# A four-layer graph attention kernel: the next unit's row spread earlier in PE's order, and the tail's masks half by DMA, half by ScalarE

## The chip, the cores and the metric

The kernel runs on one core of a Trainium2 chip. Its engines work side by side, each through its own instructions in order: TensorE (PE) multiplies matrices, VectorE (DVE), ScalarE (ACT) and GpSimd (POOL) do elementwise work, and SyncE (SP) issues nearly all DMA transfers. They wait for each other through semaphores. The metric is the time of one execution on the device in microseconds, as the median of several runs.

## The reference, in short

The input is `x`, 8 graphs of 2048 nodes with 64 features, and one adjacency matrix `adj` of 2048 by 2048. Four layers follow each other, each wrapped as `x = layernorm(x + layer(x, adj))`. Layers 0 to 2 are graph attention:

```python
h = matmul(x, W)                       # layer 0 also scales x and normalises h
s1, s2 = h @ a1, h @ a2
e = leaky_relu(s1[:, :, None] + s2[:, None, :], 0.2)
att = softmax(where(adj > 0, e, NEG_BIG), axis=-1)
out = elu(matmul(att, h))              # layer 0 adds h before the elu; layer 2 has relu
```

Layer 3 is an attention with a score of its own for every feature:

```python
feat = softplus(x * (w0 / sqrt(2)) + b0)
scores = feat * wa + ba
attn = softmax(where(mask, scores, -1e9), axis=2)
out = einsum('bijd,bjd->bid', attn, feat)
```

Because these scores don't depend on the receiving node, layer 3 is two masked sums: of exp(score) and of exp(score) times feature, over the neighbours, and their ratio.

## The kernel before, in words

**Units and tiles.** The list `todo` holds 24 units, a unit being one layer (0, 1 or 2) of one graph `b`: layers 0 and 1 of graphs 0 to 3, layers 0 and 1 of graphs 4 to 7, and then layer 2 of all eight. A unit has K = 16 tiles, one for each block of 128 sending nodes. For tile `jb`, `weights` has DVE make a weight tile `w` of 128 senders by 2048 receivers (the larger of a row and a limit, times the 0/1 edge tile); in layer 2 `exponential` then has ACT apply exp. `products` has PE multiply it with the features into the sums `acc`. There are four buffers for `w`. The text names a tile by its unit and `jb`: tile 15 is the last of a unit, "1_4" is layer 1 of graph 4.

**The row and its spread.** What DVE compares against is a row of 2048 numbers that is the same on all partitions. It lies in PSUM as `r`, in one single buffer, and `spread` writes it with four matmuls of a 3-row bf16 operand (`row3`) against ones. So the spread of the next unit must wait until DVE has read `r` for tile 15, and the first tile of the next unit (tile 0) must wait for the spread. `spread_for` does it once per unit, provided that the unit is `prepared` (its row is on its way in by DMA).

**The order of the work.** The kernel's text is run once, and every engine's instructions are kept in the order in which it emits them. The main loop goes through units `n` and tiles `jb`, and a pass is called a step here. A step calls `reach` (which emits the weights up to this tile, in layer 2 up to two tiles ahead, and the exponentials up to one ahead), then `products`, then `bg.step()`. `bg` is the side work: generators for finishing a unit (`finish`: copying `acc` to `oT`, transposing to `p_o`, dividing by `den`, normalising), for `scores` of the next layer (`p_xT`, `p_s`, `s`, `se`, `s_top`, `p_r`), for features, for the group statistics of layer 2 (`p_lse`), and for layer 3. Each goes on by one piece per step. SP's order is not fixed this way: its transfers stand in the order in which a planner expects them to become possible.

**Where the spread stood.** `reach` called `spread_for(n + 1)` as soon as it had emitted the weights of tile 15. In layers 0 and 1 that is at the start of step 15, behind the side work of step 14. In layer 2, where weights run two tiles ahead, it is in step 13, ahead of the products of tile 13.

**Layer 3 and the tail.** Graphs go in pairs. `l3_features` makes features for a graph (`sp`, `x`, `d`, `fs`, `fm`, and the high and low halves `v`), and `l3_products` goes through 64 blocks, 16 of receiving nodes for each of four pairs. A block is 32 matmuls with the mask of its nodes as the stationary operand, and ACT copies the result to `nd`. Every two blocks `l3_finish` makes the output: it loads two pieces of `e` by DMA, takes the reciprocal, multiplies (`o`), adds `e`, squares on ACT (`sq`), normalises and stores. Beside layer 2, masks come by DMA as f32 from `mask_d`, which the kernel wrote to DRAM earlier, four pieces of 256 KB for a block, in five buffers (`fetch`, asked for by `widen`). The tail is what is left when layer 2 has ended: the blocks from 33 on, with the finish of the last unit and the features of graphs 6 and 7 among them. There `widen` made a mask out of the fp8 edge matrix: ACT for the even blocks, POOL for the odd ones, in two buffers.

All engine calls pass through a helper, so that the profile has line L80 for nearly everything; the names of the tiles tell them apart.

Of the kernel before, what the change touches and what calls it, by code (L numbers as in the profile page):

```python
# [50 lines left out]
def gnn4_kernel(ctx: ExitStack, tc: tile.TileContext, t, out):  # L51
# [3 lines left out]
    K = N // P  # L55
# [51 lines left out]
    class Banks:  # L107
# [4 lines left out]
        pool = None  # L112
# [28 lines left out]
    pe, dve, act, pool = (InOrder(e) for e in (nc.tensor, nc.vector, nc.scalar, nc.gpsimd))  # L141
# [74 lines left out]
    src = t["L0_gnn_a"]  # L216
# [63 lines left out]
    def mask(p, jb):  # L280

        for h in range(2):
            dve.tensor_scalar(
                edge[:, jb, h * (N // 2) : (h + 1) * (N // 2)],
                raws[jb][h], 0.0, None, ALU.is_gt, saturate=False,
            )
        if jb < 6:
            load_raw(jb + 6)
        elif jb >= 10:
            load_raw(jb + 2)  # L290
        if jb == K2:
            load_x(2)
        if jb >= K - 3:
            load_x(jb - K + 6)
        if jb == 0:
            pe.matmul(p[:, : 2 * K], lhsT=edge[:, 0, :P], rhs=zeros_h, start=True, stop=False)
        for ib in range(K):
            pe.matmul(
                p[:, 2 * ib : 2 * ib + 2],
                lhsT=edge[:, jb, ib * P : (ib + 1) * P],  # L300
                rhs=ones_h,
                start=False,
                stop=False,
            )
        if jb == K - 1:
            pe.matmul(p[:, : 2 * K], lhsT=edge[:, 0, :P], rhs=zeros_h, start=False, stop=True)
# [504 lines left out]
    def ready(layer, b):  # L811
        return (layer, b) in V and hasattr(S.get((layer, b)), "row")
# [17 lines left out]
    def spread(layer, b):  # L830

        sc = S[layer, b]
        sc.r = Banks.r
        for c in range(NCH):
            sl = slice(c * 512, (c + 1) * 512)
            pe.matmul(sc.r[:, sl], lhsT=ones3, rhs=sc.r3[:, sl], start=True, stop=True)
# [134 lines left out]
    def unit(layer, b):  # L971
        u = Unit()
        u.layer, u.b, u.n = layer, b, f"{layer}_{b}"
        u.s, u.w = S[layer, b], {}
        return u

    def sums_of(u):
        u.acc = [psA.tile([P, 512], F32, tag="acc", name=f"acc_{u.n}_{c}") for c in range(2)]
# [5 lines left out]
    def weights(u, jb):  # L984

        s = u.s
        w = u.w[jb] = work.tile([P, N], F32, tag="w", name=f"w_{u.n}_{jb}", bufs=4)
        low = s.low if u.layer == 2 else s.e[:, 1]
        for sl in halves(u, jb):
            dve.scalar_tensor_tensor(  # L990
                w[:, sl], s.r[:, sl], low[:, jb : jb + 1], edge[:, jb, sl], ALU.max, ALU.mult
            )

    def exponential(u, jb):

        w = u.w[jb]
        for sl in halves(u, jb):
            act.activation(w[:, sl], w[:, sl], AF.Exp, bias=u.s.down[:, jb : jb + 1])

    units, prepared, spreads = [], set(), {0}  # L1000

    def spread_for(n):
        if n in spreads:
            return
        spreads.add(n)
        if n == 1:
            Banks.use("psR", 1)
            Banks.r = Banks.pool.tile([P, N], F32, tag="b", name="r")
        spread(*todo[n])
# [3 lines left out]
    def reach(t):  # L1013

        while front[0] < K * len(todo):
            n, jb = divmod(front[0], K)
            layer, b = todo[n]
            if n not in prepared or front[0] > t + (2 if layer == 2 else 0):
                break
            if jb == 0:  # L1020
                spread_for(n)
                units.append(unit(layer, b))
            weights(units[n], jb)
            front[0] += 1
            if jb == K - 1 and n + 1 in prepared:
                spread_for(n + 1)
        while behind[0] < min(front[0], t + 2):
            n, jb = divmod(behind[0], K)
            if todo[n][0] == 2:
                exponential(units[n], jb)  # L1030
            behind[0] += 1

    def products(u, jb):

        s, w = u.s, u.w[jb]
        sums = [u.acc[c // 2][F * (c % 2) : F * (c % 2) + F, :] for c in range(NCH)]
        for c in range(NCH):
            pe.matmul(
                sums[c],
                lhsT=s.v[:, jb, :],  # L1040
                rhs=w[:, c * 512 : (c + 1) * 512],
                start=(jb == 0),
                stop=False,
            )
        if jb == K - 1:

            assert s.whole
            for c in range(NCH):
                rows = slice(32 * c, 32 * c + 3)
                pe.matmul(sums[c], lhsT=s.mean[rows], rhs=emptyT[rows], start=False, stop=True)  # L1050
# [124 lines left out]
    now = [0, 0, 0]  # L1175
# [82 lines left out]
    def widen(block):  # L1258

        if block >= K * B // 2:  # L1260
            return
        ib = block % K
        src = edge[:, :, ib * P : (ib + 1) * P]
        if now[0] == 3:
            m = work.tile([P, K, P], F32R, tag="row", name=f"mask_{block}")
            if block % 2:
                pool.tensor_copy(m, src)
            else:
                act.copy(m, src)
            wide[block] = [m[:, r * K8 : (r + 1) * K8] for r in range(4)]  # L1270
            return
        wide[block] = [None] * 4
        asked.extend((block, r) for r in range(4))
# [125 lines left out]
    def chain(*gens):  # L1399
        for g in gens:  # L1400
            if isinstance(g, int):
                yield g
            else:
                yield from g()
# [26 lines left out]
    def flags():  # L1431

        for layer in range(2):
            dve.tensor_scalar(s_top[:, layer], s_top[:, layer], -S_MAX[layer], None, ALU.add)
        top = small.tile([P, 2], F32, tag="top", name="top")
        dve.tensor_reduce(top[:, 0:1], s_top, AX.XY, ALU.max)
        yield 1
        yield from pm_slots.take()
        p = psum("p_top")
        pe.transpose(p[:1, :P], top[:, 0:1], ident)  # L1440
        yield 1
        dve.tensor_reduce(top[0:1, 1:2], p[:1, :P], AX.X, ALU.max)
        pm_slots.give()
        dve.tensor_tensor(beyond[0:1, :], beyond[0:1, :], top[0:1, 1:2], ALU.max)
        dve.tensor_scalar(flag, beyond[0:1, :], 0.0, None, ALU.is_gt)
# [3 lines left out]
    for n, (layer, b) in enumerate(todo):  # L1449
        if (layer, b) == (2, 1):  # L1450
            early_.close()
            late = ctx.enter_context(tc.tile_pool(name="late", bufs=1))
            bg.add(l3_products())
        if (layer, b) == (2, 5):
            bg.add(flags())
        now[:] = layer, n, 0
        nxt = todo[n + 1] if n + 1 < len(todo) else None
        done = nxt is None

        for jb in range(K):  # L1460
            if n == 0:
                while masks < min(K, 9 + jb):
                    mask(p_deg, masks)
                    masks += 1
                if jb == K - 3:
                    empties(p_deg)
            now[2] = jb
            reach(K * n + jb)
            u = units[n]
            if jb == 0:  # L1470
                sums_of(u)
            products(u, jb)
            if jb == K - 1:
                end = [lambda u=u: finish(u)]
                if layer < 2:
                    end += [2 if now[0] < 2 else 1, lambda layer=layer, b=b: scores(layer + 1, b)]
                else:
                    end += [1, lambda b=b: l3_features(b)]
                if layer == 1 and b % NB == NB - 1:
                    end += [lambda b=b: group(b // NB)]  # L1480
                bg.add(chain(*end), begun=True)
            elif not done and jb >= 10 and ready(*nxt):
                prepare(*nxt)
                prepared.add(n + 1)
                done = True
            if layer == 0 and jb == 2 and 6 <= b + 4 < B:
                load_x(b + 4)
            if n == 0 and jb == 3:
                bg.add(constants())
            if n == 9 and jb == 3:  # L1490
                bg.add(mask_out())
            if (n, jb) in begin:
                bg.add(features0(begin[n, jb]))
            bg.step()
        while not done:
            bg.step()
            if ready(*nxt):
                prepare(*nxt)
                prepared.add(n + 1)
                done = True  # L1500
# [509 lines left out]
```

## Time and profile before

| | us |
|---|---|
| median of 3 runs | 1392.18 (1391.94 to 1396.22) |
| the profiled execution | 1391.82 |
| its span, first to last instruction | 1390.0 |
| PE busy | 1220.5 (88%) |
| DVE busy | 1214.1 (87%) |
| POOL busy | 817.7 (59%) |
| ACT busy | 751.3 (54%) |
| spread, 92 matmuls | 25.3 |
| masks cast by POOL, 16 | 30.5 |
| masks cast by ACT, 15 | 28.4 |

Times in the profile count from the first instruction. A group's row gives how many instructions there were, their busy time and mean, and the idle time of the engine just before them with what ended it. A row of the waits reads: engine and tile that waited, what it waited for, total us, number of times, longest. The chain that ended last runs from the last instruction back to whatever released each step. A matmul of f32 operands shows as several records. PE's busy time counts modelled ends, so that a busy PE isn't at its peak everywhere.

### The profile page before, as it was taken

To read this page: it belongs to the slowest core of one execution; us is meant where nothing else is said; L and a number is where in the kernel's file an instruction comes from. 1 tells how busy PE (TensorE), PEld (TensorE's weight loads), DVE (VectorE), ACT (ScalarE), POOL (GpSimd) and SP (SyncE) were. 2 spreads that over 40 slices of the span, in tenths; PEclk is the share of its full clock that TensorE was granted. 3 is DMA by queue.
4 is the path that set the end of the run, shared out by engine and by line. 5 is a ranking of instruction groups with operands and counts; after the bars stand their busy time and mean duration, and the time that the engine had idled before them with its cause. 6 is when DMAs were issued, how large, how long until landed. Compare 5 with 4: busy or idle time off the path is not lost.

```text
span 1390.0 us, 19341 instructions
## 1 busy us (share of the span) xinstructions
PE 1220.5 (88%) x7169; PEld 623.5 (45%) x7169; DVE 1214.1 (87%) x1108; ACT 751.3 (54%) x1369; POOL 817.7 (59%) x1103
## 2 busy tenths in 40 slices
PE   3689898999898979999997879799989899976996
PEld 3333233333343423343332324255644455666996
DVE  3889889999999999889999899998879798877876
ACT  4444543446245544343436987867666768564432
POOL 1566777558668686756743543343646564676665
PEclk9799999999999999999999989899999899998998
DMA  8640000000000212123101000034443444511111
GB/s 298 227 93 1 1 2 1 1 2 2 1 1 1 91 62 77 62 77 93 32 2 39 1 16 2 21 107 133 138 122 97 123 123 136 162 25 32 35 39 34
DMA packets 112010, 87.24 MB, mean 63 GB/s; under 512 B 57917, under 2 KB 90845, under 8 KB 110882
## 3 DMA queue, kind: packets, MB, share of 16 engines
q1 hardware_dynamic: 111538, 85.79, 20.6%
q8 instruction: 59, 0.97, 0.3%
q14 instruction: 45, 0.37, 0.1%
q10 hardware_dynamic: 368, 0.12, 0.0%
HBM read 60.40 MB, written 25.45 MB: 62 GB/s over the span
## 4 chain that ended last, share of the span: by engine, by line
PE 29%; DVE 15%; ACT 5%; issue 4%; POOL 2%; POOLq 0%; DVEq 0%; ACTq 0%
PE p_l L80 14%; PE acc L80 12%; DVE w L80 8%; DVE o L80 2%; ACT w L80 1%; PE p_o L80 1%; DVE nd L80 1%; DVE x L80 1%; ACT sp L80 1%; DVE fs L80 1%; PE r L80 1%; POOL sq_x L80 1%; POOL st_x L80 0%; PE p_s L80 0%; ACT L80 0%
## 5 line engine op out<-in xcount | busy, mean ns | idle before, releaser
L80 DVE SCALAR_TENSOR_TENSOR w<-r,se,edge 128x2048 f32<-128x2048 f32 (+1 forms) x270 | 552.7, 2101 | 32.2 <-PE r L80 24.5
L80 PE MATMUL acc<-w,pv 128*64 128x512 f32 x2048 | 498.9, 621 | 52.8 <-DVE w L80 41.1
L80 DVE SCALAR_TENSOR_TENSOR w<-r,lo_g,edge 128x2048 f32<-128x2048 f32 (+1 forms) x144 | 297.6, 2097 | 22.1 <-PE acc L80 12.0
L80 ACT ACTIVATE w<-w,down_g 128x2048 f32<-128x2048 f32 (+1 forms) x144 | 257.2, 1810 | 69.2 <-DVE w L80 59.7
L80 PEld LDWEIGHTS p_l<-v,mask 128*128 128x128 f32 x2048 | 256.4, 196 | 61.9 <-issue 47.8
L80 PE MATMUL p_l<-v,mask 128*128 128x256 f32 x2048 | 271.2, 291 | 10.6 <-POOL mask L80 7.0
L80 PEld LDWEIGHTS acc<-w,pv 128*64 128x64 f32 x2048 | 133.0, 139 | 312.4 <-issue 181.0
L80 PE MATMUL acc<-w,x 128*64 128x512 f32 x1024 | 259.1, 637 | 14.5 <-ACT w L80 10.8
L80 POOL TENSOR_TENSOR sq_x<-sq_x 128x32 f32<-128x32 f32 (+4 forms) x207 | 110.0, 532 | 64.8 <-ACT sq_x L80 50.3
L80 PEld LDWEIGHTS acc<-w,x 128*64 128x64 f32 x1024 | 67.0, 142 | 132.0 <-issue 89.2
L80 ACT ACTIVATE o<-p_o,den 128x64 f32<-128x64 f32 x256 | 55.9, 327 | 72.5 <-DVE den L80 72.5
L80 ACT ACTIVATE nd<-p_l,empty 128x256 f32<-128x256 f32 x64 | 30.1, 470 | 109.3 <-PE p_l L80 109.3
L80 PE MATMUL p_o<-rh,oT 128*128 128x130 f32 x384 | 60.1, 293 | 21.1 <-DVE o L80 5.8
L80 PEld LDWEIGHTS p_o<-rh,oT 128*128 128x128 f32 x384 | 49.3, 194 | 54.9 <-issue 34.3
L80 ACT COPY oT<-acc 128x512 f32<-128x512 f32 x48 | 25.6, 585 | 87.9 <-PE acc L80 87.9
L80 POOL TENSOR_TENSOR eh<-eh,x 128x1024 f32<-128x1024 f32 (+2 forms) x24 | 36.4, 1531 | 61.2 <-ACT eh L80 56.7
L80 POOL TENSOR_TENSOR st_x<-isw_x,mhalf 128x16 f32<-128x16 f32 x24 | 70.6, 2940 | 1.9
L80 POOL TENSOR_TENSOR d<-x,wa_bc 128x1024 f32<-128x1024 f32 x8 | 19.0, 2376 | 68.5 <-DVE x L80 68.5
L80 DVE RECIPROCAL nd<-nd 128x256 f32<-128x256 f32 x32 | 55.7, 1742 | 0.0
L80 POOL TENSOR_TENSOR sq_x<-o 128x512 f32<-128x512 f32 x23 | 29.3, 1272 | 41.5 <-DVE o L80 41.3
L80 ACT ACTIVATE xs<-x,nodes 128x64 f32<-128x64 f32 x128 | 44.2, 434 | 3.6 <-PE p_xT L80 3.6
L80 POOL CAST mask<-edge 128x2048 fp32r<-128x2048 fp8e4 x16 | 30.5, 1906 | 24.1 <-PE p_l L80 24.1
(260 smaller groups left out, 1558.4 us busy)
## 6 DMA issues: line engine op xcount, KB each, us to landing
mask<-mask_d SPq DMA_DIRECT2D x132, 256.0 KB
mask_d<-mf SPq DMA_DIRECT2D x32, 512.0 KB
raw<-in_adjT_dram SPq DMA_DIRECT2D x8, 1024.0 KB
raw<-in_adjT_dram SPq DMA_DIRECT2D x16, 512.0 KB
x<-in_x_dram SPq DMA_DIRECT2D x8, 512.0 KB
x_d<-x SPq DMA_DIRECT2D x8, 512.0 KB
e<-x_d SPq DMA_DIRECT2D x64, 64.0 KB
out_dram<-o SPq DMA_DIRECT2D x64, 64.0 KB
```

What stands on the lines that cost most here:

```text
L80: ins = f(*args, **kwargs)
```

## The change

Three edits. `reach` no longer emits the spread behind the weights of tile 15. The main loop does, right behind the products of one tile and ahead of that step's side work: in layers 0 and 1 behind tile 14, for which it first has `reach` emit the weights of tile 15 (at the end of layer 1 that also takes in the first two tiles of the coming unit, with their exponentials, since layer 2 runs ahead); in layer 2 behind tile 13. In the tail POOL makes no masks: the odd blocks' masks are made by ACT, and the even blocks' are asked for and fetched by DMA as beside layer 2.

```diff
@@ reach @@
             weights(units[n], jb)
             front[0] += 1
-            if jb == K - 1 and n + 1 in prepared:
-                spread_for(n + 1)
@@ widen @@
-        if now[0] == 3:
+        if now[0] == 3 and block % 2:
             m = work.tile([P, K, P], F32R, tag="row", name=f"mask_{block}")
-            if block % 2:
-                pool.tensor_copy(m, src)
-            else:
-                act.copy(m, src)
+            act.copy(m, src)
             wide[block] = [m[:, r * K8 : (r + 1) * K8] for r in range(4)]
             return
@@ the main loop @@
             products(u, jb)
+            if n + 1 in prepared and jb == K - (3 if layer == 2 else 2):
+                reach(K * n + jb + (0 if layer == 2 else 1))
+                spread_for(n + 1)
             if jb == K - 1:
                 end = [lambda u=u: finish(u)]
```

## The prediction

> **What bounds the kernel now.** I read the windows by stage first, then the chain that ended last, the groups, the waits, and for each place touched the timeline. The windows (start:end, length, then busy us of PE, PEld, DVE, ACT, POOL; clock; DMA share; GB/s) for layers 0 and 1, the last part of layer 2, the start of the tail and its steady part:
>
> ```profile
> 60.00:738.00 678.00, 623.36 (x3312) 242.37 (x3309) 629.26 (x462) 300.67 (x888) 456.20 (x622) 0.97 0.12 35
> 1017.00:1217.00 200.00, 187.22 (x1074) 109.16 (x1069) 168.14 (x167) 135.92 (x118) 112.07 (x157) 0.96 0.43 124
> 1217.00:1290.00 73.00, 52.20 (x364) 47.96 (x362) 58.05 (x77) 41.21 (x53) 50.36 (x45) 0.88 0.11 28
> 1290.00:1377.00 87.00, 86.22 (x704) 86.02 (x704) 66.82 (x118) 32.49 (x46) 54.44 (x66) 0.98 0.17 37
> ```
>
> In layers 0 and 1 VectorE (DVE) and TensorE (PE) are both near full. One tile is 2.26 us start to start on DVE, 1.87 us on PE; PE's spare time goes to side work. The tail's steady part is pure PE: 704 matmuls in 86.2 us, 3.92 us a block of 32. Before it PE idles over 20 us. The waits say what for:
>
> ```profile
> DVE w L80 <- PE r L80: 34.6, 17, 3.9
> PE r L80 <- DVE w L80: 12.9, 5, 5.0
> PE p_l L80 <- POOL mask L80: 7.0, 2, 6.2
> PE p_l L80 <- ACT mask L80: 2.4, 1, 2.4
> ```
>
> The first is DVE held at a unit's start by the spread, the second PE held in front of the spread. The group of casts that the change removes (count; busy us, mean ns of one; idle before):
>
> ```profile
> L80 POOL CAST mask<-edge 128x2048 fp32r<-128x2048 fp8e4 x16 | 30.5, 1906 | 24.1 <-PE p_l L80 24.1
> ```
>
> The tail's waits in place, with the neighbours that matter (start, duration, engine, instructions; in brackets the idle time before and its releaser):
>
> ```profile
> 1259.02 14.18 PE L80 MATMUL p_l<-v,mask 128*128 128x256 f32 x96 [6.19 <-POOL mask L80]
> 1277.20 0.43 PE L80 MATMUL p_fm<-fs,ones 128*128 128x64 f32 x2 [4.01 <-DVE fs L80]
> ...
> 1257.15 1.84 DVE L80 SCALAR_TENSOR_TENSOR st_x<-st_x 128x16 f32<-128x16 f32 x1 [2.37 <-POOL st_x L80]
> 1265.66 2.10 DVE L80 TENSOR_TENSOR o<-o,e 128x256 f32<-128x256 f32 x1
> ...
> 1257.08 1.89 POOL L80 CAST mask<-edge 128x2048 fp32r<-128x2048 fp8e4 x1
> 1265.59 1.89 POOL L80 CAST mask<-edge 128x2048 fp32r<-128x2048 fp8e4 x1 [0.31 <-PE p_l L80]
> ```
>
> A 128x16 operation took 1.84 us and ended as POOL's mask cast ended; elsewhere the same shape takes 0.15. The 128x256 one took 2.10, elsewhere 0.42. POOL's casts hold DVE, and the chain that ended last runs through just these DVE operations from 1229 to 1286.
>
> **What the Trainium skill says.** "SBUF — State Buffer", section "Who interferes with whom": a DVE instruction with two SBUF inputs and a GpSimd instruction that reads SBUF exclude each other, and whichever starts first holds the shared pair to its end. The trace agrees (1.84 against 0.15 us). The same section has DMA on ports of its own: from 920 to 1010 us mask fetches ran at 144 GB/s while PE was busy 90.00 of 90.00 us. "TensorE: Matmul & The Clock Gate", section "What's actually happening": an idle array falls to a slower clock and needs a busy stretch to recover. The block behind the 4.01 us wait took 5.56 us, not 3.92.
>
> **Spread in layers 0 and 1.** Four matmuls, 1.03 us, move ahead of the side work of step 14, with the weights of tile 15 on DVE; nothing is added, and no DMA moves with them. Of 16 unit changes, PE's order differs at eight: five are unchanged, three move only a 0.28 us mean on DVE. DVE's gap between tile 15 and the next tile 0 is 1.1 to 4.3 us, with a floor of 1.11 (at 739.60, where PE was ready). Above the floor lie 15.6 us. But side work displaced on PE is done all the same, so a gain counts only where DVE doesn't wait for PE soon after. By unit change, in order of time:
> - 0_1 to 0_2: PE was at p_mean; 0.36 us, given back at 183.43 where PE waits for POOL's tree. 0.
> - 0_2 to 0_3 and 1_5 to 1_6: 1.26 us each, but DVE's s_top soon waits for ACT's s, which is queued behind the oT copies that wait for PE's tile 15 (663.78: 1.90 us already). PE's total to there is the same. 0.
> - 1_1 to 1_2: p_xT of 1.38 us steps aside; DVE restarts at 318.2 instead of 319.53. 1.3.
> - 1_2 to 1_3: 1.03, but the next unit has no PE idle, so it returns as a wider gap at 401.86. 0.
> - 0_5 to 0_6: spread at 483.6 (tile 15's end) instead of 484.37. 0.7.
> - 0_7 to 1_4: PE now waits 0.37 for tile 15, and DVE waits for PE at 581.93 (1.81 us). A loss of 0.4.
> - 1_4 to 1_5: 32 lse matmuls (0.96) step aside; 0.9.
> - the three DVE moves: 0.3 together. In the one into layer 2, two tiles and their exponentials are also issued earlier on DVE and ACT; the mean's cast behind them waits 0.4 us at 744, covered by the 0.26 us waits that follow and oT.
> Sum: 1.3 + 0.7 - 0.4 + 0.9 + 0.3 = 2.8 us. Bounds: all of 15.6 if PE's catching up costs nothing, minus 3 if each of eight waits for tile 15 by 0.37.
>
> **Spread in layer 2.** It moves the other way, behind tile 13 (1.87 us), ahead of the side work of step 13. Where PE waited for tile 15, tile 13 fills the wait; where PE is full, the spread comes 1.87 us later and DVE's next tile with it.
> - 2_0 to 2_1: exponential 13 ends only at 779.18, so tile 13 ends at 781.07 and the spread is 0.66 later than 780.41. DVE is the chain there: a loss of 0.7.
> - 2_1 to 2_2: wait 4.30, but DVE does side work until 833.56. 0.
> - 2_2 to 2_3: wait 4.97; tile 14 must await its exponential (888.1); tile 15 and oT come 1.0 earlier, of which DVE takes its 0.57 wait for ACT's d. 0.6.
> - 2_3, 2_4 and 2_6: PE full. DVE's next tile comes 1.87 later, covered: its exponential is read at 952.6, 1015.1 and 1159.4, 4 to 7 us after it, and DVE itself then waits 2.2, 6.5 and 2.6 us for ACT's x. If that cover were gone, 1.87 each. 0.
> - 2_5 to 2_6: on the chain that ended last. Wait 1.01, then spread 1.02 and a slow tile 13 of 3.18. Tile 13's exponential was done at 1076.4, so it fills the wait; p_l starts at 1080.6 instead of 1082.9. 2.3.
> Sum: 0.6 + 2.3 - 0.7 = 2.2 us.
>
> **The tail's masks.** POOL loses 16 casts (30.5 us). ACT has 16 instead of 15, of 1.89 us, now the odd ones. SP gains 60 fetches of 256 KB, for the even ones. Where SP's fetches go: five buffers, so a fetch waits for a tile released two blocks, 7.8 us, before it is needed. Layer 2 needs a block per 7.9 us from the same five buffers, and PE's whole wait for them was 0.8 us. The rate is 1 MB per 7.84 us, 134 GB/s, plus 37 now, against 158 GB/s late in layer 2 and 298 at the start: I take its cost as nothing; the high end is in the rivals. On SP each fetch costs 0.32 us of issue, and loads and stores of the finish stand between them; the last fetches go out during blocks 60 and 61 of 63, so the last finish is untouched.
>
> What leaves: the 6.19 us wait would only become a longer wait for DVE's fs at 1277.20, since the matmul waiting there keeps its place. So the gain is what DVE gains. Casts held operations of the chain: x at 1229.06 by 0.5; st_x at 1257.15 by 1.7; o at 1265.66 by 1.7. (1.1 at 1241.60 goes to a wait for p_o.) So p_fm starts at 1277.2 - 3.9 = 1273.3. Then block 40 at the slow 5.6, block 41 without its 0.82 wait, block 42 fetched, no longer behind ACT's four casts: it starts at 1283.0 instead of 1290.28. Block 43 is new on ACT, queued behind sq, which waits for o of the finish. That is at 1293.3 now, minus 3.9, minus casts of 1.4 at 1282.21 and 1.7 at 1290.10: 1286.3; plus sq 0.4, nd 0.4, cast 1.9: 1289.0, 2.1 us after PE is ready (1286.9). Before, block 43 started at about 1294.5. Gain 5.5 us; without that new wait 7.3, with 5 us lost to lateness of fetches 0.5. From there PE sets the end in both.
>
> **Sum.** 2.8 + 2.2 + 5.5 = 10.5 us from the profiled execution's 1391.82 (span 1390.0 and 1.82 around it): 1381.3. The median of the runs shown is 0.36 above that execution: 1381.7.
>
> **Rivals.**
> - Partial (1388.5): the spread's gains all come back as waits for ACT's s, p_o or oT one step later, as they do at half of the unit changes already, and the tail gives 3.7. For it: PE idles only 2 to 5 us a unit. Against: DVE's gaps in the waits are real idle time of the busiest engine.
> - Slower (1399): fetches come late in the tail. One mechanism: SP takes its queue in order, and each block pair has a fetch behind a load of e that waits for DVE's o, or behind a store. Its margin is 7.8 us less the landing. If it is late by x, PE stalls x at each of 15 even blocks: 0.7 us eats the gain of 10.5, 1.0 us makes it slower than can be told from no change, 1.2 gives 1399. Against it: the finish has slack (DVE 66.8 of 87 us busy), and the worst such fetch that I find, the fourth of block 44 behind the loads of e at 1286.3, goes out near 1287.5 and is needed near 1296.
> - Larger (1373): PE's catching up costs little, half of the 15.6 us come, and mask 43 isn't late: 8 + 2.2 + 7.3 and about a microsecond of DVE holds.
> - The change not doing what it says: excluded for the order; for time it is the partial case.
>
> **How the numbers follow.** Forecast (1376 to 1386) 0.55, larger 0.12, partial (1386 to 1393) 0.24, slower 0.09. A difference under 0.3%, 4.2 us, can't be told from no change here. Faster (under 1388.0): 0.55 + 0.12 + 0.08 of the partial case = 0.75; slower (over 1396.4) 0.09; the rest 0.16. The range leaves out half of the larger case, the slower one and a fifth of the partial one: 1373.5 to 1391.
>
> **What would show it.** Waits of DVE w for PE r fall in layers 0 and 1 (24.5 to about 17 us), while those for ACT's s and p_o grow; in layer 2 they grow (10.1 to about 17), where they are covered. PE's waits in front of r fall from 12.9 to about 6. DVE's operations near 1257 and 1266 take 0.15 and 0.42 us. PE has no wait for POOL's mask, one of about 2 us for ACT's mask 43, and 9 us in front of p_fm. Over 1 us of waiting for the mask's DMA means the slower rival. The prediction is wrong if the tail's chain isn't DVE's, or if the time to 1217 doesn't fall.

## The result, and the profile after

The changed kernel takes 1380.24 us in the median of ten runs (1377.55 to 1384.78), the kernel before 1390.82 (1384.2 to 1396.22, ten runs beside them): a ratio of 0.9929, 95% interval 0.9913 to 0.9945, so 10.6 us less where the forecast had 10.5. The profiled execution took 1384.76 us, nearly the longest of the ten, and its span of 1383.0 is only 7.0 below the 1390.0 of before. So the two profiles can't be subtracted as wholes; they are read by stages.

The windows of the changed kernel, at the times and with the columns of the windows of before:

```profile
60.00:738.00 678.00, 621.47 (x3330) 243.96 (x3330) 632.16 (x462) 301.96 (x891) 457.90 (x626) 0.98 0.12 35
1017.00:1217.00 200.00, 187.15 (x1096) 109.77 (x1093) 170.63 (x170) 140.97 (x129) 117.37 (x161) 0.98 0.43 126
1217.00:1290.00 73.00, 54.56 (x392) 53.38 (x391) 56.82 (x90) 38.92 (x46) 40.49 (x41) 0.84 0.39 112
1290.00:1377.00 87.00, 78.77 (x653) 78.57 (x652) 57.43 (x117) 31.72 (x43) 34.77 (x57) 0.97 0.51 144
```

The last row has PE busy for 78.77 of 87 us, where it had 86.22. That isn't a slower tail, but one whose last matmul ends 78.77 us into the window, in place of 86.5. The DMA share there has gone from 0.17 to 0.51, POOL's work from 54 to 35 us.

The waits (engine and tile that waited, for what: total us, times, longest):

```profile
DVE w L80 <- PE r L80: 34.0, 17, 5.7
DVE den L80 <- PE p_o L80: 14.1, 10, 6.0
PE p_fm L80 <- DMA e<-x_d: 9.8, 1, 9.8
DVE s_top L80 <- ACT s L80: 3.3, 3, 2.2
PE p_l L80 <- ACT mask L80: 2.6, 1, 2.6
PE r L80 <- DVE w L80: 2.1, 5, 0.7
PE p_l L80 <- DMA mask<-mask_d: 0.4, 1, 0.4
```

DVE's wait for `r` is as long as before (34.0 against 34.6), but it has moved, as the two groups of weights (layers 0 and 1, then layer 2) show in their last column:

```profile
L80 DVE SCALAR_TENSOR_TENSOR w<-r,se,edge 128x2048 f32<-128x2048 f32 (+1 forms) x270 | 552.4, 2102 | 24.0 <-PE r L80 17.1
L80 DVE SCALAR_TENSOR_TENSOR w<-r,lo_g,edge 128x2048 f32<-128x2048 f32 (+1 forms) x144 | 297.3, 2096 | 25.5 <-PE r L80 16.9
```

It is 17.1 us in layers 0 and 1, from 24.5, and 16.9 in layer 2, where it is covered. PE has no wait for a mask of POOL's; it waits 9.8 us in front of the last `p_fm` and 2.6 for mask 43. (The waits put the first down to the load of `e`; PE's weight load of the same matmul, PEld, waits 10.0 for DVE's `fs`, which is what it needs.) These places in the timeline (start, duration, engine, instructions; in brackets the idle time before):

```profile
1232.42 5.76 PE L80 MATMUL p_l<-v,mask 128*128 128x256 f32 x32
1238.02 0.61 PE L80 MATMUL p_o<-rh,oT 128*128 128x130 f32 x4
...
1270.15 0.69 PE L80 MATMUL p_fm<-fs,ones 128*128 128x64 f32 x2 [9.81 <-DMA e<-x_d]
1270.15 0.50 PEld L80 LDWEIGHTS p_fm<-fs,ones 128*128 128x128 f32 x2 [10.01 <-DVE fs L80]
...
1253.43 0.17 DVE L80 SCALAR_TENSOR_TENSOR st_x<-st_x 128x16 f32<-128x16 f32 x1 [2.37 <-POOL st_x L80]
...
1260.29 0.42 DVE L80 TENSOR_TENSOR o<-o,e 128x256 f32<-128x256 f32 x1
```

The two operations that POOL's casts held take 0.17 and 0.42 us, where they took 1.84 and 2.10. But the block in front of the last unit's last `p_o` (the fourth of its four; the expectations below call it the third) took 5.76 us, not about 4, so `p_o` came later here. The next section shows why this matters.

For comparing profiles I use five marks that each of them has: the matmul that closes a unit (`acc` from `emptyT` and `mean`, here "last sum"), the last matmul of all (`p_l`), and the end of the span. The stages are A, from the second unit's last sum to that of layer 1 (unit 15, counted from 0); B, from there to that of unit 23; C, from there to the last `p_l`; D, the rest. Before: 597.5, 479.5, 155.6, 13.5. After: 595.4, 474.2, 153.9, 14.2. What lies ahead of A was 1.5 us longer in this profile. That is scatter: the first unit's last sum stands between 104.2 and 107.2 us in the profiles, whichever kernel it is, and the second unit takes 39.7 us in all of them.

### The profile page after: what moved, and what is told of

The parts are those of the page before. It is cut to its first block, busy times and chain, and to the rows that moved or that the text cites. A ratio compares the mean times of both kernels' runs of the same rounds, so it can differ in the third digit from the quotient of the medians.

```text
span 1383.0 us, 19457 instructions
## 1 busy us (share of the span) xinstructions
PE 1213.5 (88%) x7169; PEld 623.5 (45%) x7169; DVE 1200.7 (87%) x1108; ACT 753.3 (54%) x1370; POOL 790.3 (57%) x1087
## 4 chain that ended last, share of the span: by engine, by line
PE 43%; DVE 22%; ACT 7%; issue 6%; POOL 1%; DMA 0%; DVEq 0%; POOLq 0%; SPq 0%; ACTq 0%
PE acc L80 22%; PE p_l L80 14%; DVE w L80 14%; ACT w L80 2%; DVE o L80 2%; PE p_o L80 2%; PE p_s L80 1%; PE r L80 1%; ACT sp L80 1%; DVE nd L80 1%; DVE x L80 1%; PE p_lse_g L80 1%; DVE fs L80 1%; ACT L80 1%; DVE mean L80 1%
## 5 line engine op out<-in xcount | busy, mean ns | idle before, releaser
L80 DVE SCALAR_TENSOR_TENSOR w<-r,se,edge 128x2048 f32<-128x2048 f32 (+1 forms) x270 | 552.4, 2102 | 24.0 <-PE r L80 17.1
L80 PE MATMUL acc<-w,pv 128*64 128x512 f32 x2048 | 493.8, 615 | 53.8 <-DVE w L80 42.8
L80 DVE SCALAR_TENSOR_TENSOR w<-r,lo_g,edge 128x2048 f32<-128x2048 f32 (+1 forms) x144 | 297.3, 2096 | 25.5 <-PE r L80 16.9
L80 PE MATMUL acc<-w,x 128*64 128x512 f32 x1024 | 255.6, 627 | 25.3 <-ACT w L80 21.9
L80 POOL TENSOR_SCALAR isw<-isw 128x4 f32<-128x4 f32 x32 | 9.7, 302 | 105.5 <-DVE isw L80 91.8
```

The lines of the kernel that those rows point to most:

```text
L80: ins = f(*args, **kwargs)
```

## The experiments

**The three parts alone, and the whole again.** The first moves the spread of layers 0 and 1 only:

```diff
-            if jb == K - 1 and n + 1 in prepared:
+            if layer == 2 and jb == K - 1 and n + 1 in prepared:
                 spread_for(n + 1)
...
             products(u, jb)
+            if layer < 2 and n + 1 in prepared and jb == K - 2:
+                reach(K * n + jb + 1)
+                spread_for(n + 1)
```

> Only the spread of layers 0 and 1 is moved; layer 2 and the tail are as before. The theory on record: 2.8 us faster (ratio 0.998), all of it in the stretch that ends with unit 15's last sum (741.4 us before; 740.7 in the changed kernel, which had begun 1.5 later, so 2.2 shorter). A rival from the two profiles: single units moved by 4 us and back, with DVE's small operations taking 1.4 us instead of 0.3 beside POOL's work, so the stretch depends on where such collisions fall; then it may be anything from 0 to 5 us shorter, and not the same in every profile of the same order. Layer 2 from there and the tail should keep their lengths of before (479.5 us from unit 15's end to unit 23's, 169 us from there to the end).

The second moves layer 2's only:

```diff
-            if jb == K - 1 and n + 1 in prepared:
+            if layer < 2 and jb == K - 1 and n + 1 in prepared:
                 spread_for(n + 1)
...
             products(u, jb)
+            if layer == 2 and n + 1 in prepared and jb == K - 3:
+                spread_for(n + 1)
```

> Only layer 2's spread is moved, behind tile 13. The theory on record: 2.2 us faster (0.9984), nearly all between 2_5 and 2_6. The rival from the two profiles: layer 2 is 5.3 us shorter (from unit 15's last sum to unit 23's 479.5 before, 474.2 in the changed kernel), so 5 us faster (0.9962). Layers 0 and 1 and the tail keep their lengths of before.

The third has the tail's masks only:

```diff
-        if now[0] == 3:
+        if now[0] == 3 and block % 2:
             m = work.tile([P, K, P], F32R, tag="row", name=f"mask_{block}")
-            if block % 2:
-                pool.tensor_copy(m, src)
-            else:
-                act.copy(m, src)
+            act.copy(m, src)
```

> Only the tail's masks are changed: none by POOL, odd blocks by ACT, even blocks fetched. The theory on record: 5.5 us faster (0.996), from DVE's operations that POOL's casts held. The rival from the two profiles: only 1 to 2 us (0.999), because the block in front of the last unit's third p_o ran at the slow clock (5.76 us instead of about 4) and held DVE by 1.9 us, and another POOL operation held DVE by 0.9. Then from unit 23's last sum to the last matmul it is 154 us instead of 155.6.

And the whole change:

> The whole change once more, for a second profile and for the sum of the three parts on the same chip: 10.5 us by the theory on record (0.9925), measured 0.9929 so far. If the parts add, the three others give the same sum; if the moves of layers 0 and 1 change what layer 2 meets, they don't. In the profile: does the stretch of layers 0 and 1 again come out 2 us shorter, and does the block in front of the third p_o again take 5.8 us?

Measured: 0.9983 (0.9961 to 1.0005), 0.9984 (0.9968 to 1.0), 0.9995 (0.9972 to 1.0018) and, for the whole, 0.9942 (0.9924 to 0.9959). Single runs of one kernel here lie 10 us and more apart, so these intervals of 4 to 6 us don't size a part. (By medians the parts give 3.8, 1.5 and 2.1 us, 7.4 together, and the whole 9.8; with such intervals that neither shows nor excludes that the parts add.) The stages in the profiles say more. The two profiles and those of all twelve runs, the ones told further down too, in us:

| profile | A | B | C | D |
|---|---|---|---|---|
| before | 597.5 | 479.5 | 155.6 | 13.5 |
| layers 0 and 1 only | 592.9 | 477.8 | 155.3 | 13.7 |
| layer 2 only | 599.2 | 474.5 | 157.3 | 13.7 |
| tail only | 595.7 | 477.6 | 153.9 | 14.3 |
| the change | 595.4 | 474.2 | 153.9 | 14.2 |
| the change again | 592.5 | 474.0 | 150.7 | 14.2 |
| spread at 1_1 to 1_2 only | 592.2 | 476.9 | 155.3 | 13.4 |
| at the fifteen others only | 603.1 | 476.3 | 155.3 | 13.4 |
| the change, 1 of 16 spreads | 594.8 | 473.1 | 150.8 | 14.2 |
| the change, spare casts | 592.5 | 473.9 | 157.4 | 14.3 |
| the change, fetched to 43 | 593.9 | 474.5 | 158.4 | 14.2 |
| the change, all fetched | 592.6 | 474.0 | 173.2 | 14.3 |
| the change, swapped | 596.6 | 474.4 | 150.2 | 13.9 |
| swapped, again | 592.5 | 474.0 | 149.4 | 13.9 |

Stage A is 593.6 on the mean of the eight profiles with all sixteen spreads moved, and 597.5 on that of the three with none: 3.9 us. Stage B is 474.1 on the mean of nine with layer 2's moved, and 477.6 of five without: 3.5, or 3.1 if the profile of before is left out, for a reason told under layer 2. Part of the scatter is the same in every kernel: the third unit takes either 46.7 to 46.8 us or 47.7 to 49.4 between last sums, whichever kernel it is.

Stage C has two values in a kernel. One reason is the block ahead of the last `p_o`: behind the same wait of 5.2 to 5.7 us it takes 4.07 to 4.1 us in some executions and 5.6 to 5.8 in others. Without the tail's change that gives 155.3 to 155.6 and 157.3; with it 150.7 to 150.8 and 153.9. So, like against like, the change is worth 4.7 us where this block is fast (four profiles against two) and 3.4 where it is slow (one against two). Whether the change makes a slow block more likely can't be told from so few.

Block 43, behind whose start PE waits for no more masks, starts 4.7 us earlier where it is fast (behind unit 23's last sum by 69.8 to 69.9 us, which was 74.5 to 74.8) and 5.0 where it is slow (71.5, which was 76.5). From there to the last `p_l` it is 80.8 us in the five profiles without the change, 80.9 in the changed kernel's second profile and 82.4 in its first. The difference is block 43 itself. Here are block 42 of the kernel before and then block 43 of the changed kernel, in its first and its second profile, each behind PE's wait for ACT's mask (a block's end overlaps the start of the next, which comes 5.4 us behind the start of a slow block and 3.9 behind that of the other):

```profile
1290.28 5.59 PE L80 MATMUL p_l<-v,mask 128*128 128x256 f32 x32 [2.35 <-ACT mask L80]
...
1286.40 5.58 PE L80 MATMUL p_l<-v,mask 128*128 128x256 f32 x32 [2.63 <-ACT mask L80]
...
1282.11 4.09 PE L80 MATMUL p_l<-v,mask 128*128 128x256 f32 x32 [2.15 <-ACT mask L80]
```

Stage D is 0.7 us longer with fetched masks: the last store is issued 9.7 us behind the end of the last matmul in both, so the difference lies behind its issue. So the change is worth 3.9 + 3.5 + 4.7 - 0.7 = 11.4 us by stages, or 10.1 with the 3.4, and 10.6 by medians.

**One spread of sixteen, and the fifteen others.** In all profiles with the moved spread it is the unit 1_2 that is shorter, 40.0 to 40.1 us between last sums in place of 43.7 to 44.0. So I moved the spread at 1_1 to 1_2 alone, and then at all but that one:

```diff
-            if jb == K - 1 and n + 1 in prepared:
+            if not (n == 5) and jb == K - 1 and n + 1 in prepared:
                 spread_for(n + 1)
...
             products(u, jb)
+            if n == 5 and n + 1 in prepared and jb == K - 2:
+                reach(K * n + jb + 1)
+                spread_for(n + 1)
```

> The spread is moved at one unit change alone, 1_1 to 1_2, all else as before. The theory now: this one is worth nearly all that the sixteen are. Unit 1_2 (from the last sum of 1_1 to its own) takes 40.1 us, as in the three profiles with the moved spread, not 43.7 to 44.0, as in the three with the old place: 1.2 us from the earlier start (the forecast had 1.3), and the rest from two operations of DVE, mean and s, that no longer start together with one of POOL's (1.42 to 0.27 us and 2.30 to 0.94). The forecast on record had only 1.3 here. A rival: the short 1_2 comes from all the moves together (the state that earlier ones leave); then it takes 44 here.

The second has `layer < 2 and n != 5` in both places for `n == 5`.

> The spread is moved at all changes of layers 0 and 1 but 1_1 to 1_2. The theory now: unit 1_2 takes 43.7 to 44 us again, and from the last sum of the second unit to that of layer 1 no gain is left: 595 to 599 us as with the old place (597.5, 595.7 and 599.2; 592 to 595 with all moved). By the forecast on record 1.5 us of its 2.8 would remain. If the other moves are worth as much, 593 to 594 here and unit 1_2 is short as well.

Measured: 0.9982 (0.9964 to 1.0) and 1.0003 (0.9983 to 1.0023). Unit 1_2 takes 39.6 with the one and 44.05 with the fifteen; stage A is 592.2 with the one and 603.1, not shortened, with the fifteen. Layers 0 and 1 gain at one unit change above all. What happens in it, in the kernel before:

```profile
326.73 1.42 DVE L80 SCALAR_TENSOR_TENSOR mean<-mean,later,mean 128x64 f32<-128x64 bf16 x1
...
326.80 1.26 POOL L80 TENSOR_TENSOR sq_x<-sq_x 128x512 f32<-128x512 f32 x1
...
351.13 2.30 DVE L80 TENSOR_TENSOR s<-h,st_h 128x32 f32<-128x32 f32 x1
...
351.03 2.35 POOL L80 TENSOR_TENSOR o<-o,eh 128x1024 f32<-128x1024 f32 x1
```

and in the kernel with the one spread moved:

```profile
326.15 0.27 DVE L80 SCALAR_TENSOR_TENSOR mean<-mean,later,mean 128x64 f32<-128x64 bf16 x1
...
327.05 1.26 POOL L80 TENSOR_TENSOR sq_x<-sq_x 128x512 f32<-128x512 f32 x1
...
349.40 0.97 DVE L80 TENSOR_TENSOR s<-h,st_h 128x32 f32<-128x32 f32 x1
...
350.59 2.35 POOL L80 TENSOR_TENSOR o<-o,eh 128x1024 f32<-128x1024 f32 x1
```

Before, a small operation of DVE's reached its turn just as a longer one of POOL's ran, and ended with it: 1.42 us for `mean`, 2.30 for `s`. With DVE 0.8 us earlier at `mean` and 2.0 at `s`, counted from the last sum of 1_1, both come ahead of POOL and take 0.27 and 0.97. All four profiles in which this spread stands in the old place have the long pair, and all ten with it moved have the short one. An earlier `mean` of the same unit takes 0.2 us more. So the start, less this, `mean` and `s` make 1.0 - 0.2 + 1.15 + 1.3 = 3.3 us of the 4.5 between these two profiles. The rest, 1.2, comes at the unit's end, where DVE waits for the next spread for 1.63 us in place of 2.79.

Among the fifteen others one costs time, that from 0_7 to 1_4. In the kernel before, and then in the changed kernel's second profile:

```profile
571.07 1.05 PE L80 MATMUL p_s<-as,xTv 128*128 128x4 f32 x8
572.06 1.03 PE L80 MATMUL r<-row,ones 3*128 3x512 bf16 x4
573.02 1.94 PE L80 MATMUL acc<-w,pv 128*64 128x512 f32 x8
...
568.57 1.02 PE L80 MATMUL r<-row,ones 3*128 3x512 bf16 x4 [0.35 <-DVE w L80]
569.51 1.06 PE L80 MATMUL p_s<-as,xTv 128*128 128x4 f32 x8
570.50 3.32 PE L80 MATMUL acc<-w,pv 128*64 128x512 f32 x8
```

The tile behind `r` and `p_s` takes 1.94 us in the five profiles with this spread in its old place, and 2.4 to 3.6 in eight of the nine with it moved. Unit 0_7 is then 0.9 to 2.1 us longer than its 40.3. In two of them more matmuls behind it are slow too, and unit 1_4 takes 46.9 (the changed kernel's first profile) and 49.0 (the fifteen) in place of 44.15, which is 4.9 of what the fifteen's stage A is too long. That PE slows just there because it waits and then has only small matmuls is my reading; no run tests it.

**Layer 2.** By units, the five profiles of the old place and the nine of the new differ as follows: 2_0 and 2_1 together take 98.3 on the mean against 98.0 (the profile of before alone had 97.0), 2_2 to 2_4 180.4 against 179.2, and 2_5 72.9 in the profile of before, 69.8 in the four others, against 68.7. The end of 2_5 in the profile of before, the spread and what follows it:

```profile
1078.78 1.02 PE L80 MATMUL r<-row,ones 3*128 3x512 bf16 x4 [1.01 <-DVE w L80]
1079.72 3.25 PE L80 MATMUL acc<-w,x 128*64 128x512 f32 x8
```

and in that with the spread moved in layers 0 and 1 only, where layer 2 has the same order:

```profile
1077.36 1.02 PE L80 MATMUL r<-row,ones 3*128 3x512 bf16 x4
1078.31 1.94 PE L80 MATMUL acc<-w,x 128*64 128x512 f32 x8
```

The wait in front of the spread and the slow tile behind it, from which the forecast took 2.3 us, belong to that one execution. The four others have no such wait, and still the unit is 1.1 us shorter with the spread moved. It doesn't gain them at the spread of 2_5 to 2_6: in the profiles with layer 2 moved alone and with layers 0 and 1 moved alone, PE needs the same time from 15.9 us ahead of the unit's last sum on. It gains them where PE runs slowly behind a wait of 2.88 us for ACT's `w`, first with layers 0 and 1 moved only, then with layer 2 moved only:

```profile
1060.64 6.63 PE L80 MATMUL acc<-w,x 128*64 128x512 f32 x16 [2.88 <-ACT w L80]
...
1064.97 1.94 PE L80 MATMUL acc<-w,x 128*64 128x512 f32 x8 [2.88 <-ACT w L80]
1067.34 1.94 PE L80 MATMUL acc<-w,x 128*64 128x512 f32 x8 [0.43 <-ACT w L80]
```

The granted clock over these stretches is 0.54 and 1.00. Of this unit's matmuls for `acc` here, 14 are slow (over 0.9 us, where 0.6 is usual) in each of the four profiles, and in the nine none (six of them) or 6 to 8. The nine have 6 to 8 slow ones behind an earlier wait of 2.6 us, where the four have none, but there PE's next wait, 0.6 to 0.7 us in place of 2.3, takes them up. Unit 2_3 is likewise 1.3 us shorter than in the four (60.0 to 60.1 in place of 61.3 to 61.4), with as much idle time of PE, 4.1 us, and 4 to 6 slow matmuls in place of 10. So most of what layer 2 gains over these four is a shorter slow stretch of PE. That it follows the place of the spread is shown, how it does is not.

**What POOL's casts cost.** The forecast had the tail gain because POOL no longer holds DVE. To measure that by itself, POOL makes its casts again, and nobody reads them:

```diff
             act.copy(m, src)
+            pool.tensor_copy(work.tile([P, K, P], F32R, tag="row", name=f"spare_{block}"), src)
```

> The whole change, and POOL still makes its 16 casts of the odd blocks, of the same tile and shape and at their old places in its order, into buffers that nothing reads. PE waits for none of them. If POOL's casts cost the tail its time by holding VectorE, the tail is back at the length of before: 155 to 157 us from unit 23's last sum to the last matmul (150.7 to 153.9 in the three profiles with the change), and the kernel loses 3.5 us against the changed one (1384). DVE's operations then take 1.8 to 2.1 us again where a cast runs. If the gain came from PE no longer waiting for POOL's masks, or from the fetched masks, it stays (1380). ACT's masks have half as many buffers here, which a block of 3.9 us against a cast of 1.9 leaves room for.

Measured: 0.9981 (0.9965 to 0.9998), a median of 1386.03. Stage C is 157.4, although the block ahead of the last `p_o` was fast. The timeline, DVE's operations and the casts beside them:

```profile
1248.26 1.85 DVE L80 SCALAR_TENSOR_TENSOR st_x<-st_x 128x16 f32<-128x16 f32 x1 [2.37 <-POOL st_x L80]
1256.78 1.92 DVE L80 TENSOR_TENSOR o<-o,e 128x256 f32<-128x256 f32 x1
1273.15 1.85 DVE L80 TENSOR_TENSOR o<-nd 128x256 f32<-128x256 f32 x1
...
1248.18 1.89 POOL L80 CAST spare<-edge 128x2048 fp32r<-128x2048 fp8e4 x1
1256.34 2.08 POOL L80 CAST spare<-edge 128x2048 fp32r<-128x2048 fp8e4 x1
1272.83 1.89 POOL L80 CAST spare<-edge 128x2048 fp32r<-128x2048 fp8e4 x1
...
1287.00 3.25 PE L80 MATMUL p_l<-v,mask 128*128 128x256 f32 x16 [4.28 <-ACT mask L80]
```

Each of the three operations ends with its cast or 0.3 us behind it, at 1250.1, 1258.7 (the cast at 1258.4) and 1275.0 (1274.7), as the Trainium skill has it ("SBUF — State Buffer", section "Who interferes with whom"). The last `p_fm` starts 56.2 us behind unit 23's last sum, as before (56.2 to 56.3), against 53.6 without the casts, and PE's wait for mask 43 grows to 4.28 us. PE waits for none of these casts, so it is the holding, and not a wait for a POOL mask, that they cost. (One of ACT's masks waits 1.8 us for a spare cast and PE then 0.45 for that mask, both ahead of PE's wait of 12 us for `fs`, which takes them up.) Stage C is even longer than before, by 2 us: here ACT makes mask 43 behind `sq`, which itself waits for DVE, and block 43 behind the long wait takes 5.4 us.

**More fetching.** First the odd masks up to block 43 were fetched as well, against PE's wait for ACT:

```diff
-        if now[0] == 3 and block % 2:
+        if now[0] == 3 and block % 2 and block > 44:
```

> The whole change, and the odd blocks up to 43 fetched as well; from 45 on ACT makes the odd ones. The theory: PE's wait for ACT's mask 43 (2.1 to 2.7 us in three profiles) goes and nothing takes its place, so block 43 starts 67.5 to 69 us behind unit 23's last sum instead of 69.9 to 71.5, and the kernel is 2 us faster than the changed one (1378). A rival: the transfers of 12 blocks on end come later than ACT's casts did, and PE waits for them instead (waits for the mask's DMA of over 2 us), so no gain. Another: the place of the wait moves to DVE's features of the last pair, v of 4 operations, which end at 66.3: then block 48 and later wait, not block 43, and the gain stays.

And then all of the tail's, with `block < 0` in that place:

> The whole change, but all of the tail's masks fetched, none made by ACT: 1 MB per block of 3.92 us, so 267 GB/s on end. It doubles what the slower rival on record feared. If transfers can't keep that pace, PE waits for the mask's DMA: at the 144 GB/s seen beside layer 2 a block would take 7.3 us and the 21 blocks of the steady part 70 us longer; at the 290 GB/s seen in the first slice of the profile it is level and there is no loss. The theory: a loss, of 10 us or more, which shows how near the half share is to the limit.

Measured: 0.9986 (0.9972 to 1.0), a median of 1387.86 where 1378 was expected, and 1.0092 (1.0061 to 1.0124). The second's waits and its window in the tail:

```profile
PE p_l L80 <- DMA mask<-mask_d: 21.0, 22, 2.9
```

```profile
1290.00:1380.00 90.00, 78.57 (x609) 74.15 (x608) 42.92 (x97) 12.33 (x29) 27.82 (x47) 1.00 0.85 253
```

The slower rival exists: 253 GB/s is what came, with DMA busy for 0.85, and two blocks take about 9.5 us instead of 7.7. Fetching only to block 43 brought 11.7 us of such waits, nine of them, although what came there is far below 253 GB/s: 168 GB/s over the first 71.6 us of stage C. So the rival that its expectation names came true. In this stretch SP's queue has loads of `e` and stores, which wait for DVE, between the fetches; I take that for the reason, but no run tests it by itself, nor whether more than five buffers would help. With ACT making every other mask there is a whole block more of time, and PE waits 0.4 us.

**The two sources exchanged.** ACT makes the even blocks, the odd ones are fetched:

```diff
-        if now[0] == 3 and block % 2:
+        if now[0] == 3 and block % 2 == 0:
```

> The whole change with the two sources exchanged: ACT makes the even blocks, the odd ones are fetched. Nothing of POOL's or DVE's changes, so DVE's chain to p_fm and to the last features is the same. The mask that stands behind the features' casts on ACT is then 42 or 44 in place of 43. The theory: within 1 us of the changed kernel (1380). If the order on ACT is what the tail hangs on, PE's waits for ACT's masks go from 2.1 to 2.7 us to 4 or to nothing, and the time with it.

Measured: 1378.49 in the median of six runs, 0.9919 (0.9903 to 0.9936). Again, since that is below the changed kernel:

> The kernel with the two sources exchanged once more, since its six runs had a median 1.7 us below the changed kernel's, with intervals that overlap (0.9919, 0.9903 to 0.9936, against 0.9929 and 0.9942). In its profile the tail from unit 23's last sum to the last matmul took 150.2 us although the block ahead of the third p_o ran slowly; the changed kernel took 153.9 in that state and 150.7 in the other. If that holds, this profile has 150.2 or, with a fast block, 148 to 149, PE's wait for ACT's mask is 1.3 us instead of 2.1 to 2.7, and the ratio is again 0.990 to 0.993. If it was the luck of one profile, the tail is 151 to 154 and the ratio 0.994.

Measured: 1377.22, 0.9915 (0.9896 to 0.9934). The waits of PE in it:

```profile
PE p_fm L80 <- DVE fs L80: 7.3, 1, 7.3
...
PE p_l L80 <- DMA mask<-mask_d: 2.1, 2, 1.0
PE p_l L80 <- ACT mask L80: 1.1, 1, 1.1
```

Stage C is 149.4 with a fast block ahead of the last `p_o` and 150.2 with a slow one (150.7 and 153.9 in the changed kernel). Mask 42, made by ACT, keeps PE for 1.1 to 1.3 us where mask 43 kept it for 2.2 to 2.7, and the block behind that wait takes 3.9 us in both profiles, never 5.4. The median of all twelve runs is 1377.75 us, 2.5 below the changed kernel's. The intervals of the two overlap, so that it beats the changed kernel is likely, not proven; it beats the kernel before.

**Fifteen spreads put back.** The whole change with only the spread at 1_1 to 1_2 moved in layers 0 and 1:

```diff
             front[0] += 1
+            if layer < 2 and n != 5 and jb == K - 1 and n + 1 in prepared:
+                spread_for(n + 1)
...
-            if n + 1 in prepared and jb == K - (3 if layer == 2 else 2):
+            if n + 1 in prepared and (n == 5 or layer == 2) and jb == K - (3 if layer == 2 else 2):
```

> The whole change, but of the sixteen spreads of layers 0 and 1 only that from 1_1 to 1_2 is moved. The theory: the same time as the changed kernel (1380), since that one move carried the gain (592.2 us from the second unit's last sum to that of layer 1 with it alone, 593.4 on the mean of five profiles with all, 603.1 and 0 gain without it). If the fifteen others do harm, as the single profile of 603.1 against 597.5 hints, it is 3 to 5 us faster than the changed kernel.

Measured: 1380.48, 0.9943 (0.9927 to 0.9958): the changed kernel's time. If the fifteen together help or harm, it is by no more than the 2 us to either side that this interval leaves open.

## Why the prediction was right, and where it wasn't

The total was right to 0.1 us in the difference and 1.5 in the time. That close an agreement is luck: the interval of the measured difference is some 2 us to either side, and three terms of the sum were mis-sized, with errors that cancel. The mechanism was right for the tail, right but not carried far enough for layers 0 and 1, and for layer 2 not the one that brings most of the gain.

**Spread in layers 0 and 1: 2.8 forecast, 3.9 measured.** The step for 1_1 to 1_2 was right as far as it went: DVE restarts 1.2 us earlier, forecast 1.3 (at 318.76 in the profile with this spread alone, which ran 0.5 later up to A, for 319.53). What failed is that it stopped there. An earlier start was priced by itself, when it also decides which of DVE and POOL comes first at the next places where they meet; two such places, and a shorter wait at the unit's end, turned 1.0 into 4. The 0.7 at 0_5 to 0_6 came to nothing. The 0.9 at 1_4 to 1_5 came (1_5 takes 41.25 us in place of 42.1 to 42.9), but 0_7 to 1_4 lost more than the forecast 0.4, which is what it costs in the one profile whose tile behind the spread stays fast; the slow tile was in no step. The signs: waits for `r` fell to 17.1 as forecast, those for `p_o` grew (8.8 to 14.1; 10.6 in the second profile), those for ACT's `s` did not (3.2, 3.3), and PE's in front of `r` fell further than forecast (2.1, not 6).

**Spread in layer 2: 2.2 forecast, 3.5 measured.** DVE's wait for `r` grew to 16.9 as forecast, and was covered as forecast. The 2.3 of 2_5 to 2_6 came out of a wait and a slow tile that four other profiles of the same order don't have; there the unit gains 1.1, and not at that spread. The loss of 0.7 at 2_0 to 2_1 agrees with the one profile of before (1.0 in the two units) but not with the others, where it is a gain or nothing. And 2_2 to 2_4 give 1.2, not 0.6. So the waits that this term rested on are not what brings the gain. Most of it comes from shorter slow stretches of PE, which were in no step.

**The tail: 5.5 forecast, 4.0 or 2.7 measured, by the execution.** The mechanism was right, and the spare casts show it: POOL's casts hold DVE's chain, the three holds vanish, PE stands 9.8 us in front of `p_fm` (forecast 9) and 2.2 to 2.7 for mask 43 (forecast 2.1). The term "p_fm starts 3.9 earlier" was mis-sized: it is 2.6 to 2.8. A freed POOL doesn't stand still, and its next operations, the low halves `v`, now meet DVE:

```profile
1239.35 3.29 DVE L80 SCALAR_TENSOR_TENSOR o<-o,x 128x1008 f32<-128x1008 f32 x2
...
1239.08 1.30 POOL L80 TENSOR_TENSOR v<-x,v 128x512 fp32r<-128x512 f32 x1 [2.19 <-ACT v L80]
1240.33 2.26 POOL L80 TENSOR_TENSOR v<-d,v 128x512 fp32r<-128x512 f32 x1
```

The pair of DVE operations took 2.41 us before. Half a microsecond more went the same way further on, where POOL's `e` waits for its load and then holds one `v` of DVE (1.23 us, its like 0.63 to 0.68). The other way went the start of block 43 in the kernel before: the forecast put it at about 1294.5, 4.2 us behind that of block 42, since it had read 3.92 us a block. That is the mean of 22 blocks, of which block 42, behind its wait, took 5.4 and the others 3.84; block 43 started at 1295.7. Together that leaves block 43 4.7 to 5.0 earlier, not 5.5. "From there PE sets the end in both" left out that block 43 itself, behind its new wait, can run slowly, which cost 1.5 us in two of the four profiles. And the 0.7 of stage D was in no step; why the end comes later behind fetched masks stays open.

**The rivals.** Larger needed half of 15.6 us from the spreads; it is a quarter. Partial had the spread's gains all come back: true of fifteen unit changes taken together, not of the sixteenth. Slower was far off with half of the masks fetched (0.4 us of waits), and its mechanism appears as soon as more are.

## What to carry to other kernels

Where two engines hold each other, an edit that shifts one of them by a microsecond is worth what it does to every later meeting of the two, so look for the operations of one engine that end together with the other's, and ask which of them the shift parts or joins. Work that is taken off an engine is best priced by putting it back with nobody reading it. A wait or a slow tile seen in one execution is no base for a term until a second execution shows it too. And where PE waits for microseconds, ask what a changed order does to its pace behind the wait.

## What the runs showed of the hardware

A wait of 5.2 to 5.7 us in front of PE was followed by 16 matmuls in 3.5 to 3.8 us, where 16 matmuls of a steady block take 1.9, and then by a block of 32 that took 4.07 to 4.1 us in some executions and 5.6 to 5.8 in others, with the same instructions in the same order. That PE comes back at half its pace agrees with the Trainium skill ("TensorE: Matmul & The Clock Gate", section "What's actually happening"). One block more or less of it comes and goes between executions, and is worth 1.7 us each time.

Behind PE's wait for a mask of ACT's in front of block 42 or 43, the block was followed by the next after 5.2 to 5.4 us in the eight profiles with a wait of 2.3 us or more, and after 3.9 in the four with 2.2 or less. In the kernel before the granted clock was 0.68 over such a slow block and 1.00 over the next. Between the changed kernel's two profiles the wait differs by 0.5 us and the block behind it by 1.5. That the length of the wait decides is not shown; behind the same 2.88 us in layer 2, PE's clock was 0.54 in a profile of one order of its work and 1.00 in one of the other.

Fetches came at 253 GB/s beside PE's matmuls, where masks had come at 144 GB/s over 90 us of layer 2; I had not expected that.
